# Softmax row sums of an attention kernel: partial sums folded by DMA onto half of the partitions, and a product with ones over half of the columns

## The chip, the cores and the metric

One core of one Trainium2 chip. The metric is the device time of one execution in microseconds; three runs of the kernel before took 2589.92 to 2592.28 us, median 2590.79 us. The profile is of one execution that took 2589.98 us, of which the program's instructions span 2588.2 us.

## The reference

The input is `x`, 4 images of 128 channels with 64 x 64 pixels, in float32. Two layers follow each other:

```python
# layer 0: attention over the 4096 pixels of an image, 4 heads of 32 channels
x_norm = group_norm(x, 8 groups)
q, k, v = split(qkv_w @ x_norm + qkv_b), each to [image, head, pixel, 32]
attn = softmax(q @ k.T * 32 ** -0.5)          # [image, head, 4096, 4096]
x = x + proj_w @ (attn @ v) + proj_b
# layer 1: two 3x3 convolutions with 3-bit weights
out = relu(batch_norm(conv3x3(x, quantize(w1))))
out = batch_norm(conv3x3(out, quantize(w2)))
x = relu(out + x)
```

A softmax row is exp(score) divided by the sum of exp(score) over 4096 keys. The change concerns how these sums are made.

## The kernel before

Attention runs in 32 blocks, one for each image and each 512 of its queries (`FB = 512`). A block has 32 steps, one for each 128 keys. In a step, `scores` makes for two pairs of heads the scores of 128 keys (on the partitions) against 512 queries into PSUM (L425), and ScalarE writes their exponentials into one of eight buffers of the tile `p`, 128 x 4 heads x 512 (L427). `weights` multiplies them with the values into `acc`, four heads on four bands of 32 partitions (L438). The scores run ahead of the weights: an outer loop gives three half-steps of scores, then one step of weights, then three, then two.

The sums over the keys are made in two stages. First, the exponentials of all 32 steps are added element by element into one tile of the same shape, so that each partition holds the sum over its own 32 keys. For 26 steps VectorE does that, into `r` (L448 and L450). For six, those in `MOVED = (4, 9, 14, 19, 24, 28)`, a DMA issued by GpSimd does it, into the tile `rm`: the first of a block copies (L443), the others accumulate (L445). Each moves 1 MB, on all 128 partitions. In the next block, after step 1, `merge` accumulates `rm` onto `r` by one more such DMA (L471). There is one buffer of `rm`, so the first copy of a block waits for the merge of the block before.

Then `sums` adds over the 128 partitions, by a product with a matrix of ones on TensorE (L467): one for each head and each half of the columns, eight in all, each of 256 columns. It leaves the sum of a head on all 32 partitions of its band in the tile `l`, and ScalarE copies that to SBUF (`ls`, L475). One float32 product is two records in the profile.

From there `spread` sends one row of each head to 128 partitions, `invert` takes the reciprocals there and writes them to DRAM, `gather` reads them back onto the bands, and `weigh` multiplies them with the block's output; `project` and `store` end the block.

`schedule` says after which step of the next block each of these parts is put out. Its `slots` are every third step; one visit to a slot puts other work between two groups of attention products. The sums of a block take slot 3, or slots 3 and 4 with half of the columns each; in seven blocks (`full`: the six that also project two chunks of the next image, and block 1) both halves go to slot 3. The last block has no next one, and takes `sums_at_once`, which multiplies `rm` and `r` with ones without merging them.

GpSimd issues, in program order on one queue, these accumulating DMAs as well as the stores of the projected keys, queries and values of the next image to DRAM (`kd`, `qd`, `vd`, L340 and L359) and of finished blocks (`y`, L525). A wait of one of them holds all that come after it. [...]

Of the kernel before, what the change touches and what calls it, by code (L numbers as in the profile page):

```python
# [16 lines left out]
F32 = mybir.dt.float32  # L17
AF = mybir.ActivationFunctionType
ALU = mybir.AluOpType
# [3 lines left out]
P = 128  # L23
GROUP = 16
HEADS = 4
D = 32
TAPS = 9
FB = 512
# [50 lines left out]
def _fast_body(ctx, tc, x, norm_w, norm_b, qkv_wt, qkv_b, proj_wt, proj_b,  # L79
               w1, alpha1, gamma1, beta1, w2, alpha2, gamma2, beta2, out, cnt):  # L80
    nc = tc.nc
# [10 lines left out]
    const = ctx.enter_context(tc.tile_pool(name="const", bufs=1))  # L92
# [19 lines left out]
    nc.scalar.activation(warm, mhalf, AF.Exp)  # L112
    ones = const.tile([P, D], F32, name="ones")
    nc.gpsimd.memset(ones, 1.0)
    worst = const.tile([P, FB // D], F32, name="worst")
    nc.gpsimd.memset(worst, 0.0)
    nw, nb = column(norm_w, "nw"), column(norm_b, "nb")
# [84 lines left out]
    dram = ctx.enter_context(tc.tile_pool(name="dram", bufs=1, space=bass.MemoryType.DRAM))  # L202
    kpool = ctx.enter_context(tc.tile_pool(name="kpool", bufs=NB + 1))
    pss = ctx.enter_context(tc.tile_pool(name="pss", bufs=3, space=PSUM))
    psa = ctx.enter_context(tc.tile_pool(name="psa", bufs=2, space=PSUM))
# [3 lines left out]
    att = ExitStack()  # L209
    vpool = att.enter_context(tc.tile_pool(name="vpool", bufs=NB + 1))  # L210
    qpool = att.enter_context(tc.tile_pool(name="qpool", bufs=2))
    stage = att.enter_context(tc.tile_pool(name="stage", bufs=1))
    xpool = att.enter_context(tc.tile_pool(name="xpool", bufs=3))
    ppool = att.enter_context(tc.tile_pool(name="ppool", bufs=8))
    rpool = att.enter_context(tc.tile_pool(name="rpool", bufs=1))
    sums = att.enter_context(tc.tile_pool(name="sums", bufs=2))
    wpool = att.enter_context(tc.tile_pool(name="wpool", bufs=1))

    def stack_tile(name):
# [8 lines left out]
    def load_x(b, j):  # L228
        t = xpool.tile([P, FB], F32, name=f"x{b}_{j}", tag="x")
        nc.sync.dma_start(out=t, in_=x_chunk(b, j))  # L230
        return t
# [64 lines left out]
    def banded(out, w, x):  # L296


        for c in range(HEADS):
            cs = slice(c * D, (c + 1) * D)  # L300
            nc.tensor.matmul(out[cs, :], w[:, cs], x, start=True, stop=True)  # L301
# [107 lines left out]
    pts, acc, rsum, msum = {}, {}, {}, {}  # L409
    MOVED = (4, 9, 14, 19, 24, 28)  # L410
# [20 lines left out]
    def weights(step):  # L431
        n, kt = divmod(step, NK)
        v = vs[blocks[n][0], kt // KB]
        pt = pts[step]
        if kt == 0:
            acc[n] = psa.tile([P, FB], F32, name=f"acc{n}", tag="a")
        for h in range(HEADS):
            nc.tensor.matmul(acc[n][h * D : (h + 1) * D, :], v[:, kt % KB, h * D : (h + 1) * D],  # L438
                             pt[:, h, :], start=(kt == 0), stop=(kt == NK - 1))
        if kt in MOVED:  # L440
            if kt == MOVED[0]:
                msum[n] = rpool.tile([P, HEADS, FB], F32, name=f"rm{n}", tag="rm")
                nc.gpsimd.dma_start(out=msum[n], in_=pt)  # L443
            else:
                nc.gpsimd.dma_start(out=msum[n], in_=pt, accum_op=ALU.add)  # L445
        elif kt == 1:
            rsum[n] = sums.tile([P, HEADS, FB], F32, name=f"r{n}", tag="r")
            nc.vector.tensor_tensor(rsum[n], pts[step - 1], pt, ALU.add)  # L448
        elif kt > 1:
            nc.vector.tensor_tensor(rsum[n], rsum[n], pt, ALU.add)  # L450

    def finish_parts(n):

        b, qb = blocks[n]
        av = rpool.tile([P, FB], F32, name=f"av{n}", tag="av")
        rc = rpool.tile([P, FB], F32, name=f"rc{n}", tag="rc")
        t = {}

        def copy():
            nc.scalar.copy(av, acc[n])  # L460


        def total(r, first, end, cs=slice(0, FB)):
            if "l" not in t:
                t["l"] = psa.tile([P, FB], F32, name=f"l{n}", tag="a")
            for h in range(HEADS):
                nc.tensor.matmul(t["l"][h * D : (h + 1) * D, cs], ones, r[:, h, cs],  # L467
                                 start=first, stop=end)

        def merge():  # L470
            nc.gpsimd.dma_start(out=rsum[n], in_=msum[n], accum_op=ALU.add)  # L471

        def evacuate():
            t["ls"] = stage.tile([P, FB], F32, name=f"ls{n}", tag="ls")
            nc.scalar.copy(t["ls"], t["l"])  # L475

        def sums(i):
            total(rsum[n], True, True, slice(i * FB // 2, (i + 1) * FB // 2))
            if i == 1:
                evacuate()  # L480


        def sums_at_once():
            total(msum[n], True, False)
            total(rsum[n], False, True)
            evacuate()
            for j in range(4):
                cs = slice(j * P, (j + 1) * P)
                nc.vector.reciprocal(rc[:, cs], t["ls"][:, cs])
            weigh()  # L490
            most = [small.tile([P, 1], F32, name=f"most{i}") for i in range(2)]
            for u, m in zip((t["ls"], rc), most):
                nc.vector.tensor_reduce(m, u, AX.X, ALU.max)
                nc.vector.tensor_tensor(worst[:, 0:1], worst[:, 0:1], m, ALU.add)

        def spread():
            t["lq"] = rpool.tile([P, FB // D], F32, name=f"lq{n}", tag="lq")
            nc.sync.dma_start(out=t["lq"], in_=t["ls"][0:P:D, :])  # L500

        def invert():
            t["rq"] = rpool.tile([P, FB // D], F32, name=f"rq{n}", tag="rq")
            nc.vector.reciprocal(t["rq"], t["lq"])
            t["rd"] = dram.tile([HEADS, FB], F32, name=f"rd{n}")
            nc.sync.dma_start(out=t["rd"].rearrange("h (j c) -> (h j) c", c=FB // D), in_=t["rq"])
            nc.vector.tensor_tensor(worst, worst, t["lq"], ALU.add)
            nc.vector.tensor_tensor(worst, worst, t["rq"], ALU.add)

        def gather():  # L510
            nc.sync.dma_start(out=rc, in_=t["rd"].unsqueeze(1).to_broadcast([HEADS, D, FB]))

        def weigh():
            nc.vector.tensor_tensor(av, av, rc, ALU.mult)

        def residual():
            t["x"] = load_x(b, qb)

        def project():
            t["o"] = psa.tile([P, FB], F32, name=f"po{n}", tag="a")  # L520
            banded(t["o"], wp, av)

        def store():
            nc.vector.scalar_tensor_tensor(t["x"], t["o"], bp, t["x"], ALU.add, ALU.add)
            nc.gpsimd.dma_start(out=y0[b][:, qb * FB : (qb + 1) * FB], in_=t["x"])  # L525

        return dict(copy=copy, merge=merge, sums=sums, sums_at_once=sums_at_once, spread=spread, invert=invert, gather=gather,
                    weigh=weigh, residual=residual, project=project, store=store)

# [64 lines left out]
    def schedule(n, before):  # L594
        b, qb = blocks[n]
        todo = []
        slots = [kt for kt in range(NK - 1) if (n * NK + kt) % 3 == 0]
        two = b + 1 < B and qb in (2, 3)
        full = two or n == 1

        def add(kt, f):
            todo.append((kt, f))

        def visit(kts, first, second, evacuate=None):
            add(kts[0], first)
            add(kts[-1], second)
            if evacuate:
                add(kts[-1] + 1, evacuate)

        if before:  # L610
            add(1, before["merge"])
            kts = slots[3:4] if full else slots[3:5]
            visit(kts, lambda: before["sums"](0), lambda: before["sums"](1))
            kt = kts[-1]
            add(kt + 1, before["spread"])
            add(kt + 3, before["invert"])
            add(kt + 4, before["gather"])
            add(kt + 6, before["residual"])
            add(slots[9] - 2, before["weigh"])
            add(slots[9], before["project"])  # L620
            add(slots[9] + 1, before["store"])
# [69 lines left out]
    def run_weights(count):  # L691
        for _ in range(min(count, steps - at["step"])):
            n, kt = divmod(at["step"], NK)
            if kt == 0:
                assert not todo
                todo[:] = schedule(n, parts.get(n - 1))
            weights(at["step"])
            at["step"] += 1
            if kt == NK - 2:
                parts[n] = finish_parts(n)  # L700
            if kt == NK - 1:
                parts[n]["copy"]()
            else:
                side(kt)
# [135 lines left out]
    for b in range(B):  # L840
        for j in range(4):
            y = res[b, j]
            cs = slice(j * HN, (j + 1) * HN)
# [462 lines left out]
```

## Time and profile before

| | |
|---|---|
| median of 3 runs | 2590.79 us |
| TensorE busy | 2517.2 us, 97% of the span |
| VectorE busy | 2140.3 us, 83% |
| ScalarE busy | 2081.9 us, 80% |
| GpSimd busy | 281.4 us, 11% |
| attention | to about 2270 us; then the convolutions |
| accumulating DMAs on `rm` (L445) | 160, 7.9 us from issue to landing, median of all 192 on `rm` |
| merging DMAs (L471) | 31, 7.1 us |
| product with ones (L467) | 504 records, 37.9 us of TensorE |

Busy time is the time in which an engine has at least one instruction under way, so instructions that overlap count once; a mean duration is that of one instruction alone. Behind the bar, a group shows the idle time of its engine just before its instructions, and who ended most of it. The share of a DMA queue is the time that its packets took, over 16 DMA engines and the stretch looked at.

### The profile page before, as it was taken

To read this page: it belongs to the slowest core of one execution; us is meant where nothing else is said; L and a number is where in the kernel's file an instruction comes from. 1 tells how busy PE (TensorE), PEld (TensorE's weight loads), DVE (VectorE), ACT (ScalarE), POOL (GpSimd) and SP (SyncE) were. 2 spreads that over 40 slices of the span, in tenths; PEclk is the share of its full clock that TensorE was granted. 3 is DMA by queue.
4 is the path that set the end of the run, shared out by engine and by line. 5 is a ranking of instruction groups with operands and counts; after the bars stand their busy time and mean duration, and the time that the engine had idled before them with its cause. 6 is when DMAs were issued, how large, how long until landed. Compare 5 with 4: busy or idle time off the path is not lost.

```text
span 2588.2 us, 48399 instructions
## 1 busy us (share of the span) xinstructions
PE 2517.2 (97%) x20394; PEld 1223.4 (47%) x20394; DVE 2140.3 (83%) x1402; ACT 2081.9 (80%) x2275; POOL 281.4 (11%) x456
## 2 busy tenths in 40 slices
PE   6999999999999999999999999999999999999894
PEld 3444444444444444444444444444444444477773
DVE  5898888888988898888988988888999998953344
ACT  4888899999988999999988899999889898911223
POOL 2111111111011111110011111110000000100000
PEclk9999999999999999999999999999999999999997
DMA  5876766698667767697667666986655757634004
GB/s 160 191 187 172 177 161 149 154 206 201 162 148 178 178 155 171 149 225 171 160 171 161 164 159 150 207 202 142 151 130 126 154 126 148 146 80 145 1 1 164
DMA packets 147417, 400.04 MB, mean 155 GB/s; under 512 B 59240, under 2 KB 60008, under 8 KB 118648
## 3 DMA queue, kind: packets, MB, share of 16 engines
q0 software_dynamic: 45888, 280.59, 47.9%
q1 hardware_dynamic: 100728, 115.23, 16.8%
q8 instruction: 162, 2.65, 0.4%
q10 hardware_dynamic: 576, 1.05, 0.1%
q14 instruction: 63, 0.52, 0.1%
HBM read 105.32 MB, written 55.83 MB: 62 GB/s over the span
## 4 chain that ended last, share of the span: by engine, by line
PE 88%; DVE 5%; issue 3%; DMA 2%; ACT 1%; POOL 0%; SPq 0%; DVEq 0%; POOLq 0%; ACTq 0%
PE s L425 39%; PE acc L438 34%; PE c L722 9%; DVE r L450 3%; DMA rm<-p 2%; PE l L467 1%; PE po L301 1%; PE pk L301 1%; PE pq L301 1%; PE pv L301 1%; ACT p L427 1%; DVE res L844 1%; DMA xh<-in_x_dram 0%; DMA q<-qst 0%; DVE st L570 0%
## 5 line engine op out<-in xcount | busy, mean ns | idle before, releaser
L427 ACT ACTIVATE p<-s 128x1024 f32<-128x1024 f32 x2048 | 1940.2, 1034 | 235.0 <-PE s L425 158.7
L450 DVE TENSOR_TENSOR r<-r,p 128x2048 f32<-128x2048 f32 x768 | 1758.4, 2290 | 97.3 <-ACT p L427 48.1
L425 PE MATMUL s<-q,k 64*128 64x512 f32 x8192 | 1162.3, 413 | 3.9 <-ACT p L427 2.2
L438 PE MATMUL acc<-p,v 128*32 128x512 f32 x8192 | 1021.1, 601 | 0.6 <-DVE v L355 0.6
L425 PEld LDWEIGHTS s<-q,k 64*128 64x128 f32 x8192 | 711.7, 185 | 631.9 <-issue 298.0
L438 PEld LDWEIGHTS acc<-p,v 128*32 128x32 f32 x8192 | 198.6, 109 | 453.7 <-issue 446.3
L445 POOL DMA_DIRECT2D rm<-p x160 | 138.6, 866 | 950.7 <-ACT p L427 783.6
L775 ACT COPY cv<-c 128x512 f32<-128x512 f32 x64 | 37.6, 587 | 220.8 <-DVE st L774 220.8
L722 PE MATMUL c<-hi,wq 128*128 128x512 f32 x576 | 150.1, 405 | 8.3 <-DVE hi L805 6.8
L722 PE MATMUL c<-lo,wq 128*128 128x512 f32 x576 | 148.1, 402 | 0.0
L774 DVE BATCH_NORM_STATS2 st<-c 128x6 f32<-128x512 f32 x64 | 44.7, 699 | 124.5 <-PE c L722 102.5
L722 PEld LDWEIGHTS c<-hi,wq 128*128 128x128 f32 x576 | 109.4, 191 | 40.1 <-issue 8.9
L722 PEld LDWEIGHTS c<-lo,wq 128*128 128x128 f32 x576 | 109.0, 189 | 28.9
L448 DVE TENSOR_TENSOR r<-p,p 128x2048 f32<-128x2048 f32 x32 | 73.3, 2291 | 25.0 <-ACT p L427 25.0
L336 DVE SCALAR_TENSOR_TENSOR kst<-pk,b,kst 128x512 fp32r<-128x512 f32 x32 | 24.0, 751 | 73.2 <-ACT kst L335 73.2
L336 DVE SCALAR_TENSOR_TENSOR qst<-pq,b,qst 128x512 fp32r<-128x512 f32 x32 | 24.0, 750 | 41.6 <-ACT qst L335 41.6
L471 POOL DMA_DIRECT2D r<-rm x31 | 26.3, 848 | 159.8 <-PE s L425 91.9
L340 POOL DMA_DIRECT2D qd<-qst x31 | 23.3, 753 | 177.6 <-DVE qst L336 130.2
L443 POOL DMA_DIRECT2D rm<-p x32 | 17.8, 556 | 223.3 <-ACT p L427 136.4
L335 ACT ACTIVATE kst<-pk,b 128x512 fp32r<-128x512 f32 x32 | 22.4, 701 | 21.7 <-PE pk L301 21.7
L340 POOL DMA_DIRECT2D kd<-kst x28 | 20.6, 734 | 167.6 <-DVE kst L336 159.6
L467 PE MATMUL l<-r,ones 128*32 128x256 f32 (+1 forms) x504 | 37.9, 383 | 0.5 <-issue 0.5
(129 smaller groups left out, 672.0 us busy)
## 6 DMA issues: line engine op xcount, KB each, us to landing
rm<-p POOLq DMA_DIRECT2D x192, 1024.0 KB, 7.9
q<-qd SPq DMA_DIRECT2D x248, 128.0 KB
r<-rm POOLq DMA_DIRECT2D x31, 1024.0 KB, 7.1
x<-in_x_dram SPq DMA_DIRECT2D x80, 256.0 KB
k<-kd SPq DMA_DIRECT2D x124, 128.0 KB
qd<-qst POOLq DMA_DIRECT2D x31, 512.0 KB, 6.9
kd<-kst POOLq DMA_DIRECT2D x28, 512.0 KB, 4.0
y<-x POOLq DMA_DIRECT2D x32, 256.0 KB, 5.0
```

Of the source, the lines that this page charges most:

```text
L301: nc.tensor.matmul(out[cs, :], w[:, cs], x, start=True, stop=True)
L336: nc.vector.scalar_tensor_tensor(lo, ps[what], bias, t[:, 0, :], ALU.add, ALU.subtract)
L340: (nc.sync if start else nc.gpsimd).dma_start(out=dst[b, j].rearrange("s p n -> p s n"), in_=t)
L425: nc.tensor.matmul(s[:, i, :], k[r, half, c0 : c0 + P], q[r, half, part, :], start=(part == 0), stop=(part == 1))
L427: nc.scalar.activation(pts[step][:, 2 * half : 2 * half + 2, :], s, AF.Exp, scale=SCALE)
L438: nc.tensor.matmul(acc[n][h * D : (h + 1) * D, :], v[:, kt % KB, h * D : (h + 1) * D], pt[:, h, :], start=(kt == 0), stop=(kt == NK - 1))
L445: nc.gpsimd.dma_start(out=msum[n], in_=pt, accum_op=ALU.add)
L448: nc.vector.tensor_tensor(rsum[n], pts[step - 1], pt, ALU.add)
L450: nc.vector.tensor_tensor(rsum[n], rsum[n], pt, ALU.add)
L467: nc.tensor.matmul(t["l"][h * D : (h + 1) * D, cs], ones, r[:, h, cs], start=first, stop=end)
L722: nc.tensor.matmul(ps[:, j, :].rearrange("p (r w) -> p r w", w=W), w[:, tap, :], part[:, j * RB + kh : j * RB + kh + RB, kw : kw + W], sta ...
L774: nc.vector.bn_stats(st[:, b * NB + c, :], ps[:, j, :])
```

## The change

The partial sums of the DMAs no longer keep the shape of `p`. Their new tile `f` has 128 partitions and two blocks of 512 columns in place of four: the lower 64 partitions hold heads 0 and 2, the upper 64 hold heads 1 and 3, and each partition holds the sum of two partitions of `p`. `fold` brings a tile there in four DMAs of 256 KB (64 partitions, two heads): first each half of the partitions with its own two heads, then each half of the partitions from the other one. The second two of a fold wait for the first two. `f` has two buffers. `merge` now folds `r` into `f` in the same way, where it added `rm` onto `r` before.

With two heads on two halves of the partitions, one product of 256 columns with `pair` (ones in the upper left and the lower right quarter, zeros elsewhere) makes the sums of two heads at a time. Four products, one to a band, make all sums of a block: a band holds two heads, 16 partitions each, for one half of the columns. So the copy to `ls` has 256 columns, `spread` takes one row out of every 16 partitions, and the reciprocals come back in two transfers. All blocks make their sums in one visit, at slot 3. The last block multiplies `f` with `hones` (ones on one half of the partitions) and `r` with `ones`.

```diff
+    hones = const.tile([P, 2, D], F32, name="hones")
+    pair = const.tile([P, D], F32, name="pair")
+    for t in (hones, pair):
+        nc.gpsimd.memset(t, 0.0)
+    for i in range(2):
+        r = slice(i * P // 2, (i + 1) * P // 2)
+        nc.gpsimd.memset(hones[r, i, :], 1.0)
+        nc.gpsimd.memset(pair[r, i * D // 2 : (i + 1) * D // 2], 1.0)
...
+    fpool = att.enter_context(tc.tile_pool(name="fpool", bufs=2))
...
         if kt in MOVED:
-            if kt == MOVED[0]:
-                msum[n] = rpool.tile([P, HEADS, FB], F32, name=f"rm{n}", tag="rm")
-                nc.gpsimd.dma_start(out=msum[n], in_=pt)
-            else:
-                nc.gpsimd.dma_start(out=msum[n], in_=pt, accum_op=ALU.add)
+            fold(n, pt)
...
+    def fold(n, t):
+        new = n not in msum
+        if new:
+            msum[n] = fpool.tile([P, 2, FB], F32, name=f"f{n}", tag="f")
+        rows = [slice(i * P // 2, (i + 1) * P // 2) for i in range(2)]
+        for first in (True, False):
+            for r in range(2):
+                src = t[rows[r if first else 1 - r], r::2, :]
+                if new and first:
+                    nc.gpsimd.dma_start(out=msum[n][rows[r]], in_=src)
+                else:
+                    nc.gpsimd.dma_start(out=msum[n][rows[r]], in_=src, accum_op=ALU.add)
...
         def merge():
-            nc.gpsimd.dma_start(out=rsum[n], in_=msum[n], accum_op=ALU.add)
+            fold(n, rsum[n])
...
-        def sums(i):
-            total(rsum[n], True, True, slice(i * FB // 2, (i + 1) * FB // 2))
-            if i == 1:
-                evacuate()
+        def sums():
+            l = psa.tile([P, FB], F32, name=f"l{n}", tag="a")
+            for c in range(4):
+                f, i = divmod(c, 2)
+                nc.tensor.matmul(l[c * D : (c + 1) * D, : FB // 2], pair,
+                                 msum[n][:, i, f * FB // 2 : (f + 1) * FB // 2],
+                                 start=True, stop=True)
+            t["ls"] = stage.tile([P, FB], F32, name=f"ls{n}", tag="ls")
+            nc.scalar.copy(t["ls"][:, : FB // 2], l[:, : FB // 2])
...
-            nc.sync.dma_start(out=t["lq"], in_=t["ls"][0:P:D, :])
+            nc.sync.dma_start(out=t["lq"], in_=t["ls"][0 : P : D // 2, : FB // 2])
...
-            nc.sync.dma_start(out=rc, in_=t["rd"].unsqueeze(1).to_broadcast([HEADS, D, FB]))
+            for f in range(2):
+                nc.sync.dma_start(out=rc[:, f * FB // 2 : (f + 1) * FB // 2],
+                                  in_=t["rd"][f].unsqueeze(1).to_broadcast([HEADS, D, FB // 2]))
...
-            kts = slots[3:4] if full else slots[3:5]
-            visit(kts, lambda: before["sums"](0), lambda: before["sums"](1))
-            kt = kts[-1]
+            kt = slots[3]
+            add(kt, before["sums"])
```

More of the change, by code (lines that the diff above doesn't have):

```diff
@@ L460, in copy, with merge, sums_at_once @@
             nc.scalar.copy(av, acc[n])
-        def total(r, first, end, cs=slice(0, FB)):
-            if "l" not in t:
-                t["l"] = psa.tile([P, FB], F32, name=f"l{n}", tag="a")
-            for h in range(HEADS):
-                nc.tensor.matmul(t["l"][h * D : (h + 1) * D, cs], ones, r[:, h, cs],
-                                 start=first, stop=end)
-        def merge():
-            nc.gpsimd.dma_start(out=rsum[n], in_=msum[n], accum_op=ALU.add)
-        def evacuate():
-            t["ls"] = stage.tile([P, FB], F32, name=f"ls{n}", tag="ls")
-            nc.scalar.copy(t["ls"], t["l"])
-        def sums(i):
-            total(rsum[n], True, True, slice(i * FB // 2, (i + 1) * FB // 2))
-            if i == 1:
-                evacuate()
[L483 to L486, printed above, removed]
+        def merge():
+            fold(n, rsum[n])
[8 more added lines that the diff above has]
+            nc.scalar.copy(t["ls"][:, : FB // 2], l[:, : FB // 2])
+        def sums_at_once():
+            l = psa.tile([P, FB], F32, name=f"l{n}", tag="a")
+            for h in range(HEADS):
+                nc.tensor.matmul(l[h * D : (h + 1) * D, :], hones[:, h % 2, :], msum[n][:, h // 2, :],
+                                 start=True, stop=False)
+            for h in range(HEADS):
+                nc.tensor.matmul(l[h * D : (h + 1) * D, :], ones, rsum[n][:, h, :],
+                                 start=False, stop=True)
+            t["ls"] = stage.tile([P, FB], F32, name=f"ls{n}", tag="ls")
+            nc.scalar.copy(t["ls"], l)
             for j in range(4):
@@ L504, in invert @@
             nc.vector.reciprocal(t["rq"], t["lq"])
-            t["rd"] = dram.tile([HEADS, FB], F32, name=f"rd{n}")
-            nc.sync.dma_start(out=t["rd"].rearrange("h (j c) -> (h j) c", c=FB // D), in_=t["rq"])
+            t["rd"] = dram.tile([2, HEADS, FB // 2], F32, name=f"rd{n}")
+            nc.sync.dma_start(out=t["rd"].rearrange("f h (j c) -> (f h j) c", c=FB // D), in_=t["rq"])
             nc.vector.tensor_tensor(worst, worst, t["lq"], ALU.add)
@@ L598, in schedule @@
         two = b + 1 < B and qb in (2, 3)
-        full = two or n == 1
         def add(kt, f):
```

## The prediction

> **What bounds the kernel now.** I read the page first (busy shares, then the chain that ended last), then busy time by stretch, then the order of time on TensorE around the row sums, and last the tile `rm` and the DMA queues over short stretches.
>
> The page: shares, chain, groups.
>
> ```profile
> PE 2517.2 (97%) x20394; PEld 1223.4 (47%) x20394; DVE 2140.3 (83%) x1402; ACT 2081.9 (80%) x2275; POOL 281.4 (11%) x456
> ...
> PE 88%; DVE 5%; issue 3%; DMA 2%; ACT 1%; POOL 0%; SPq 0%; DVEq 0%; POOLq 0%; ACTq 0%
> ...
> L427 ACT ACTIVATE p<-s 128x1024 f32<-128x1024 f32 x2048 | 1940.2, 1034 | 235.0 <-PE s L425 158.7
> ...
> L445 POOL DMA_DIRECT2D rm<-p x160 | 138.6, 866 | 950.7 <-ACT p L427 783.6
> ...
> L467 PE MATMUL l<-r,ones 128*32 128x256 f32 (+1 forms) x504 | 37.9, 383 | 0.5 <-issue 0.5
> ```
>
> Busy time by stretch, from the middle of attention:
>
> ```profile
> 300.00:700.00 400.00, 400.00 (x3422) 179.30 (x3416) 353.01 (x194) 363.11 (x395) 46.97 (x62) 1.00 0.75 176
> 1500.00:1900.00 400.00, 399.54 (x3346) 176.50 (x3342) 358.80 (x221) 362.06 (x392) 43.36 (x57) 1.00 0.72 164
> ```
>
> TensorE has no gap, ScalarE and VectorE have about a tenth free, and the DMA engines are taken for about 0.73 of the time. So a product taken off TensorE shortens attention, as long as nothing else fills up.
>
> TensorE in order of time, one visit that makes all sums of a block and one that makes half of them:
>
> ```profile
> 767.64 1.06 PE L438 MATMUL acc<-p,v 128*32 128x512 f32 x8
> 768.52 1.05 PE L467 MATMUL l<-r,ones 128*32 128x256 f32 x16
> 769.50 1.66 PE L425 MATMUL s<-q,k 64*128 64x512 f32 x12
> ...
> 1740.98 0.61 PE L467 MATMUL l<-r,ones 128*32 128x256 f32 x8
> 1741.53 1.67 PE L425 MATMUL s<-q,k 64*128 64x512 f32 x12
> ```
>
> The pipe gives 0.98 us (768.52 to 769.50) to 16 records and 0.55 us (1740.98 to 1741.53) to 8.
>
> The tile `rm` (the time of its DMAs to landing, and who waited for it):
>
> ```profile
>   ACT p L427: 4.1, 5
> ...
> DMA to landing us min/median/max: 4.4/7.8/14.6
> ```
>
> The DMA queues: first over 300 to 2200 us, then 745.9 to 754 us (one accumulating transfer alone), 754 to 761 us (one plain one alone), and 22.6 to 23.15 us (start-up copies from 32 partitions of SBUF to 32 others). Columns: packets, MB, share of 16 engines.
>
> ```profile
> q0 software_dynamic: 37682, 237.04, 55.6%
> q1 hardware_dynamic: 52023, 73.76, 15.2%
> ```
>
> ```profile
> q0 software_dynamic: 144, 1.05, 64.4%
> ...
> r<-rm POOLq DMA_DIRECT2D x1, 1024.0 KB, 7.6
> ```
>
> ```profile
> q0 software_dynamic: 144, 1.05, 38.8%
> ...
> rm<-p POOLq DMA_DIRECT2D x1, 1024.0 KB, 4.6
> ```
>
> ```profile
> q1 hardware_dynamic: 48, 0.07, 48.8%
> ```
>
> 64.4% of 8.1 us is 5.2 us of all 16 engines for 1 MB accumulated; 38.8% of 7 us is 2.7 us for 1 MB copied. Accumulating costs twice a copy[...]. 128 data packets of 8 KB make 0.34 us a packet for the copy, 0.085 us for each 2 KB. The start-up copies moved 32 packets of 2 KB: 48.8% of 0.55 us times 16, over 32, is 0.134 us each, 1.6 times as long.
>
> [...] 16 engines times 2 KB in 0.134 us is 245 GB/s, against 385 GB/s at 0.085 us. [...] No transfer of the kernel before shows an accumulation on half of the partitions.
>
> **The change part by part.**
>
> *Products removed.* Sums of 31 blocks go from eight products (16 records) to four (8 records). Seven blocks ("full": six with two chunks, and block 1) did them in one visit and save 0.98 - 0.55 = 0.43 us each, 3.0 us. The other 24 did them in two visits of 0.55 us and save one, 13.2 us. All lies on TensorE, which sets the end: -16.2 us. The last block has as many products as before.
>
> *ScalarE copy of `ls`.* Half the columns of a 0.6 us copy, 31 times: about 9 us on an engine with a tenth free. Nothing.
>
> *Constants, spread, gather.* Six more small memsets at the start, of 0.1 to 0.2 us as those beside them, ahead of `nw` and `wqkv`, which the program needs some 14 us later. The reciprocals travel as before in 8 KB; they are read back by two transfers instead of one, and `weigh` comes about twelve steps (some 27 us) later. Nothing.
>
> *Waits on TensorE.* The sums now wait for two landings, and stand where the first half stood before, which needed the merged tile as well.
>
> *The DMA sums.* Each fold (six per block, and the merge) was one transfer of 1 MB; it is four of 256 KB, in two phases. Phase A adds a half onto itself: source and destination both on 64 partitions. Phase B adds the other half, and waits for A's landing. Bytes are the same. GpSimd issues four: between 0.5 (start-up) and 0.85 us each, so up to 3.4 us of a fold interval of some 10 us: no bound by itself. In order of time:
>
> - A reads 512 KB per transfer[...] 2.1 us at the measured 245. The lower bound is the engines' own 1.3 us (5.2 / 4). I take 2.2.
> - B reads its source from one half and its destination from the other: 1.3 us if they interleave[...]. [...]I take 1.4.
> - A fold is 2 x 2.2 + 2 x 1.4 = 7.2 us of all engines in place of 5.2 (from 5.2 to 9.6).
> - 300 to 2200 us holds 27 blocks of 7: 189 folds. 2.0 us more each is 378 of 1900 us, 20 points: DMA share from 71 to 91%. It fits, with little left.
>
> Latency: from issue the first packet comes after about 1.4 us. A1 stands behind A0 on the same engines; with one part in seven for other traffic (5.2 us of data plus about 1.9 fixed is 7.1, the median is 7.8), A0 ends at 3.9 us and A1 at 6.4; B0, issued at about 4.2, follows A1 at once and ends at 8.0; B1, issued at 6.6, ends at 9.6. About 10 us to landing in place of 7.8. A probability tile has eight buffers: with 6.9 us per three steps and a visit (768.52 to 775.41) it is written again 18 us after its exps start, some 15.5 us after they end. So 5 us of room stay, less what GpSimd is behind. Queued behind the waiting phase B on GpSimd are the stores of k, q, v and y: up to 6 us later, and needed by loads many steps later. The chain itself can start a fold every 8 us or so, and folds come every 9 to 11. The merge is issued at 746.11 and the sums stand at 768.52: 22 us for 10. One wait goes away: two buffers of `f` mean that the first fold of a block no longer waits for the merge.
>
> I charge 3 us for folds that come late in the blocks with the most stores. Sum: -16.2 + 3 = -13 us, **2577.5 us**.
>
> **Rivals.**
>
> *DMA full.* If A takes 2.4 and B 1.8, a fold is 8.4 us and the share 71 + 189 x 3.2 / 19 = 103%. Then folds set the pace of attention (2200 us): 3% over, and bubbles between phases on top, +65 to +100 us less the 16 gained: about 2660. If B too takes 2.4: 71 + 44 = 115%, 2900. [...]
>
> *Room for p used up.* Folds fit on average, but GpSimd runs behind where stores, merge and fold meet; ScalarE then waits for a landing (before: 4.1 us in all, 5 times), and TensorE for ScalarE. Some 1 us for each of 30 to 45 of 223 folds: 2605 to 2620. For it: the longest landing was already 14.6 us of 15.5. Against it: the median has 5 us left.
>
> *No change.* ScalarE's wait and TensorE's gain cancel, 2590. Narrow.
>
> **How the numbers follow.** Forecast 0.50, room used up 0.20, DMA full 0.23, no change 0.07. Faster is the forecast alone: 0.50. Slower is two rivals: 0.43. The range starts under the full 16 us with a little from ScalarE, 2569, and takes in the room rival and the lower part of the full one, to 2680; some 0.12 stay above it, for A and B both near 2.4.
>
> **What would show it.** Right: `l` with 8 records a block (about 250), near 0.55 us for each; folds landing in about 10 us from their first issue; ScalarE waiting for `f` under 15 us in all; DMA share about 0.9 between 300 and 2200 us; TensorE without gaps. Wrong: ScalarE waiting for `f` by hundreds of us, TensorE with gaps before `s`, DMA share at 1.0 and folds landing later and later in a block. If the share stays near 0.75, [...] my A is too high.

## The result, and the profile after

The changed kernel takes 2846.87 us (median of 4 runs, 2843.37 to 2855.29), the kernel before 2590.85 us (4 runs) in the same session: a ratio of 1.099 with a 95% interval of 1.097 to 1.102. It is 256 us slower, where 13 us less were forecast.

The page of the changed kernel: busy shares, the chain that ended last, and two of its groups.

```profile
PE 2594.7 (91%) x20146; PEld 1221.0 (43%) x20146; DVE 2143.3 (75%) x1402; ACT 2075.0 (73%) x2275; POOL 947.4 (33%) x1131
...
DMA 53%; PE 28%; issue 10%; POOL 4%; ACT 3%; DVE 2%; SPq 0%; POOLq 0%; ACTq 0%; DVEq 0%
DMA f<-p 49%; PE s L435 10%; PE acc L448 8%; PE c L743 8%; DMA f<-r 4%; POOL f L470 3%; ACT p L437 2%; DVE r L456 1%; POOL f L468 1%; DVE res L865 1%; PE po L311 0%; PE pk L311 0%; PE pq L311 0%; PE pv L311 0%; DMA wqkv<-in_L_conv_qkv_w_dram 0%
...
L435 PE MATMUL s<-q,k 64*128 64x512 f32 x8192 | 1208.1, 421 | 182.3 <-ACT p L437 178.8
L470 POOL DMA_DIRECT2D f<-p x704 | 684.0, 977 | 1343.9 <-DMA f<-p 1219.5
```

Before, the chain was TensorE for 88% and DMA for 2%. Now DMA is 53%, nearly all of it `f<-p`, the folds (one fold is the four transfers that bring one tile into `f`). GpSimd stands 1219.5 us in front of accumulating transfers, waiting for the landing of an earlier one, and TensorE stands 178.8 us in front of scores because ScalarE has not freed a PSUM tile.

Busy time by stretch, the same two as before the change:

```profile
300.00:700.00 400.00, 369.68 (x3076) 160.81 (x3072) 315.27 (x174) 321.96 (x352) 152.62 (x168) 0.97 0.91 158
1500.00:1900.00 400.00, 368.39 (x3074) 161.25 (x3068) 311.70 (x172) 318.56 (x348) 151.19 (x166) 0.96 0.91 156
```

All three compute engines have lost some 8 to 13% of their busy time in each stretch, so none of them sets the pace. The DMA engines are at 0.91, not at 1. The DMA queues of 300 to 2200 us agree with 73.9 and 14.9%:

```profile
q0 software_dynamic: 105532, 214.67, 73.9%
q1 hardware_dynamic: 50096, 68.86, 14.9%
```

How the wait travels, in the list of waits of the whole program (who waited for whom, us in total, times, longest):

```profile
POOL f L470 <- DMA f<-p: 1255.6, 593, 6.7
...
ACT p L437 <- DMA f<-p: 211.4, 72, 9.5
...
PE s L435 <- ACT p L437: 178.8, 101, 9.1
```

GpSimd issues a fold late because the fold before has not landed; the tile of `p` that it reads is therefore released late; ScalarE, which wants to write that buffer again, waits (before: 4.1 us in 5 waits); TensorE waits for ScalarE.

A0 and A1 are the two transfers of a fold's first phase, A, and B0 and B1 those of its second, each written to the same half as the A of its number. From each transfer's issue and landing, a fold looks like this in the median: A0 is issued at 0 and lands at 5.3 us; B0, which waits for it, is issued at 5.66 and lands at 9.76; the next fold of the block, whose A0 waits for that, starts at 10.25. In the mean, which is what counts over a block, A0 lands after 5.7 us, B0 goes out 0.3 us later and lands after 4.6 more, and the next A0 goes out 0.5 us after that: 11.1 us from fold to fold. Seven of them are 78 us; before, a block took 67 to 73 us from the third on (from its first exps to those of the next). That the mean is the chain's own length, and not a pace set elsewhere, shows in how seldom it breaks: of 222 folds that follow another, 172 were issued within 0.7 us of the landing of the B0 before them, and 28 sooner, each the first of its block, which writes the other buffer of `f`; only 22 came later. Before, 94 of 222 were issued so soon after a landing, and folds came 10.0 us apart in the mean.

So GpSimd falls behind. In the median of the 192 folds of `p` it issued A0 5.0 us after the exps that the fold reads had ended (before, 0.6 us), and the whole fold had landed 17.9 us after these exps (before, 9.0). The prediction had counted some 15.5 us until the buffer of `p` is written again.

Of the 31 blocks compared, 27 got 3 to 14 us longer. In blocks 7, 15 and 23 (counted from 0) the DMA engines also load the next image's keys and values; these got 20, 22 and 13.5 us longer.

### The profile page after: what moved, and what is told of

The parts are those of the page before. It is cut to its first block, busy times and chain, and to the rows that moved or that the text cites. A ratio compares the mean times of both kernels' runs of the same rounds, so it can differ in the third digit from the quotient of the medians.

```text
span 2842.5 us, 49017 instructions
## 1 busy us (share of the span) xinstructions
PE 2594.7 (91%) x20146; PEld 1221.0 (43%) x20146; DVE 2143.3 (75%) x1402; ACT 2075.0 (73%) x2275; POOL 947.4 (33%) x1131
## 4 chain that ended last, share of the span: by engine, by line
DMA 53%; PE 28%; issue 10%; POOL 4%; ACT 3%; DVE 2%; SPq 0%; POOLq 0%; ACTq 0%; DVEq 0%
DMA f<-p 49%; PE s L435 10%; PE acc L448 8%; PE c L743 8%; DMA f<-r 4%; POOL f L470 3%; ACT p L437 2%; DVE r L456 1%; POOL f L468 1%; DVE res L865 1%; PE po L311 0%; PE pk L311 0%; PE pq L311 0%; PE pv L311 0%; DMA wqkv<-in_L_conv_qkv_w_dram 0%
## 5 line engine op out<-in xcount | busy, mean ns | idle before, releaser
L435 PE MATMUL s<-q,k 64*128 64x512 f32 x8192 | 1208.1, 421 | 182.3 <-ACT p L437 178.8
L470 POOL DMA_DIRECT2D f<-p x704 | 684.0, 977 | 1343.9 <-DMA f<-p 1219.5
L448 PE MATMUL acc<-p,v 128*32 128x512 f32 x8192 | 1063.2, 623 | 2.2 <-DVE x L547 1.6
L470 POOL DMA_DIRECT2D f<-r x124 | 120.6, 976 | 188.4 <-DMA f<-r 135.9
L795 DVE BATCH_NORM_STATS2 st<-c 128x6 f32<-128x512 f32 x64 | 44.7, 699 | 124.7 <-PE c L743 101.9
L559 POOL MEMSET t<- 128x18 f32 x32 | 5.9, 184 | 177.1 <-PE c L743 107.6
L468 POOL DMA_DIRECT2D f<-p x64 | 51.0, 977 | 0.2 <-issue 0.2
L350 POOL DMA_DIRECT2D kd<-kst x28 | 29.1, 1039 | 29.5 <-DVE kst L346 28.8
L350 POOL DMA_DIRECT2D qd<-qst x31 | 33.0, 1076 | 11.7 <-DVE qst L346 11.7
```

Of the source, the lines that this page charges most:

```text
L350: (nc.sync if start else nc.gpsimd).dma_start(out=dst[b, j].rearrange("s p n -> p s n"), in_=t)
L435: nc.tensor.matmul(s[:, i, :], k[r, half, c0 : c0 + P], q[r, half, part, :], start=(part == 0), stop=(part == 1))
L468: nc.gpsimd.dma_start(out=msum[n][rows[r]], in_=src)
L470: nc.gpsimd.dma_start(out=msum[n][rows[r]], in_=src, accum_op=ALU.add)
L795: nc.vector.bn_stats(st[:, b * NB + c, :], ps[:, j, :])
```

## The experiments

Two theories, each seeming enough by itself. P, partitions: a transfer that reads both inputs of its addition, source and destination, from one half of the partitions is slow. C, chain: the second phase of a fold waits for the first, and that puts two issues and two landings in a row. A third, S, is that many small transfers cost as such. Each run stood beside a run of the kernel before on the same chip; where no interval is given, it is one run, and differences are tens of us.

**All partitions.** Only the slices in `fold` change:

```diff
-                src = t[rows[r if first else 1 - r], r::2, :]
+                src = t[:, r if first else r + 2, :]
...
-                    nc.gpsimd.dma_start(out=msum[n][rows[r]], in_=src, accum_op=ALU.add)
+                    nc.gpsimd.dma_start(out=msum[n][:, r, :], in_=src, accum_op=ALU.add)
```

> The same four transfers of 256 KB in a fold, the same two phases with the same wait between them, the same 2 KB pieces; but each transfer now goes over all 128 partitions (head r of p onto column block r, then head r + 2 onto the same block). The row sums so made mix heads; number of bytes, issues, products and waits are those of the change. Theory P[...]: folds shrink from a period of 10.25 us to 7 or 8, TensorE is the bound again, 2575 to 2600 us. Theory C (chain: two phases one after the other, each with a fixed cost of issue and landing, set the length[...]): no change, 2820 to 2860 us.

Measured: 2638.42 us. Neither theory alone: transfers over all partitions take back 208 us of the 256, and 47 us are left over 2591.47. ScalarE's waits for the tile fall from 211.4 us to 44.7:

```profile
ACT p L437 <- DMA f<-p: 44.7, 15, 7.3
```

The terms of the chain are now 4.4, 0.5, 4.1 and 0.5 us in the mean (the last where a fold still waits for the one before; 97 of 222 now come later than that). Seven times 9.5 us are 66 us, which is close to a block. 19 of the 31 blocks are no longer than before, and half of the loss lies in blocks 7, 15 and 23 with their loads; in the change one block of 31 was no longer.

**Own half twice, other half twice.** `src = t[rows[r], r::2, :]` in both phases, and `src = t[rows[1 - r], r::2, :]` in both.

> Both phases of a fold read their source from the half of the partitions that they write (phase A twice); the other half's partitions are left out of the DMA sums, and their own are counted twice. P: phase B gets as slow as phase A (5.3 us from issue to landing in place of 4.1), a fold period near 11.5 to 12 us, 3000 to 3150 us. C: 2820 to 2870 us, as the change.

> Both phases read their source from the other half (phase B twice)[...]; each half's own partitions are left out of the DMA sums. P: phase A gets as fast as phase B (4.1 us), a fold period near 9 us, 2600 to 2700 us. C: 2820 to 2860 us, as the change.

Measured: 3074.73 us and 2684.94 us, as P has it in both. Between 300 and 2200 us the median 2 KB packet on GpSimd's queue took 336 ns with the own half, 191 with the other half, 187 over all partitions. So reading two inputs from one half is slow, and reading one from each half costs almost nothing in the packets. Folds started 12.1, 10.4 and 10.2 us apart in the mean, against 11.1 in the change and 10.0 before. Most of what the halves cost is in phase A: without it, 162 of the 208 us are gone.

**No wait between the phases.** Phase B adds onto a tile of its own:

```diff
+            cross[n] = gpool.tile([P, 2, FB], F32, name=f"g{n}", tag="g")
...
-        for first in (True, False):
+        for dst, first in ((msum[n], True), (cross[n], False)):
```

> Phase B adds onto a tile of its own, so that it no longer waits for phase A; same transfers from and to the same halves. The tile of phase B is left out of the row sums. The first phase B of a block is a copy, which saves a little. P alone: the transfers take what they took, the engines stay full, 2780 to 2850 us. C: the chain per fold is half as long (5 us in place of 10), TensorE is the bound again, 2575 to 2620 us. Something in between says that the wait costs because it comes on top of slow transfers.

The lines left out write `dst` in place of `msum[n]`, and let the first phase B of a block be a copy.

Measured: 2613.96 us. The same slow transfers, from and to the same halves, cost 22 us over the kernel before when a phase does not wait for the other. Its busy time by stretch:

```profile
300.00:700.00 400.00, 395.59 (x3344) 174.92 (x3340) 347.37 (x192) 356.36 (x388) 165.83 (x184) 1.00 0.95 171
1500.00:1900.00 400.00, 398.28 (x3320) 175.03 (x3320) 357.79 (x214) 360.79 (x394) 163.89 (x181) 1.00 0.94 167
```

The DMA engines are busier here (0.95) than in the change (0.91), and TensorE is nearly full. So it was not the DMA engines' share that held the change up: they could carry these transfers at almost the old pace, though one in fourteen is a copy here that is an addition in the change. Nor was it the length of one fold: from first issue to last landing it took 12.4 us in the median here, and 12.2 in the change.

**Both remedies.** All partitions, and the second phase on its own tile.

> Both remedies at once, to complete the two by two: all 128 partitions in each transfer, and the second phase on a tile of its own, so nothing waits within a fold (the sums mix heads, and the second tile is left out of them). Products, number of issues, bytes and pieces are those of the change. [...] the gain of the products alone, 2576 to 2584 us. If four issues a fold, or something else of the change, costs as well: 2590 us or more.

Measured: 2582.80 us, ratio 0.997 (0.996 to 0.998), within 4 us of the products alone (below). That completes the two by two:

| | phase B waits for phase A | no wait |
|---|---|---|
| halves of the partitions | 2847 (the change) | 2614 |
| all partitions | 2638 | 2583 |

From the lower right, the halves alone add 31 us, the wait alone 56, both together 264, three times their sum. The numbers above fit one reading: with the wait alone seven folds need 66 us, which most blocks have and those with more traffic do not; with halves and wait they need 78, which hardly any has. ScalarE's waits for landings go the same way: 6 us with neither, 25 with the halves alone, 45 with the wait alone, 211 with both.

**Four transfers, no phases.** The kernel before, each 1 MB transfer cut into four of one head each:

```diff
-                nc.gpsimd.dma_start(out=msum[n], in_=pt, accum_op=ALU.add)
+                for h in range(HEADS):
+                    nc.gpsimd.dma_start(out=msum[n][:, h, :], in_=pt[:, h, :], accum_op=ALU.add)
```

> The kernel before with each 1 MB transfer cut into four of 256 KB, one for each head, on all 128 partitions; no second phase, nothing waits within a fold, old products. If four issues and 2 KB pieces cost by themselves (theory S): 2610 to 2640 us, as much as full ports with two phases did. If the wait between phases is what costs there: 2588 to 2598 us, as before.

Measured: 2591.41 us, beside 2591.21. S falls: four issues and 2 KB pieces are hidden here, although GpSimd is busy for 147 us of 400 in place of 47.

**The products alone.** The old transfers and merge, the new products on the merged tile:

```diff
-                                 msum[n][:, i, f * FB // 2 : (f + 1) * FB // 2],
+                                 rsum[n][:, i, f * FB // 2 : (f + 1) * FB // 2],
```

> The kernel before, its transfers of 1 MB and its merge, with the new products alone: four of 256 columns in one visit, on the merged tile's first two heads (heads 2 and 3 and the upper half's share are left out of the sums), and the shorter copy and the new spread and gather. It measures what the product is worth with nothing lost to the transfers. If TensorE sets the pace: 16 us less, 2573 to 2578 us. If ScalarE or VectorE already share the pace: 2583 to 2592 us.

Measured: 2579.13 us, ratio 0.9953 (0.9937 to 0.997): 12 us less, with an interval of 8 to 16. The tile `l` in this run:

```profile
L481 PEld LDWEIGHTS l<-r,pair x248: 105/110/111, 138.2 to 2213.0; 128*32 128x32 f32 x124
L481 PE MATMUL l<-r,pair x248: 376/379/404, 138.2 to 2213.2; 128*32 128x256 f32 x124
```

248 records are eight for each of 31 blocks. Before, there were sixteen for each, 496, and eight of the last block under the same line, 504. Most blocks are 0.2 to 0.4 us shorter than before.

**Four folds in place of six.** `MOVED = (4, 11, 18, 25)`, and VectorE adds two more steps of a block.

> The change with four folds for the steps of a block in place of six (steps 4, 11, 18, 25), so five with the merge; VectorE adds the two others, 2.3 us each. If a block waits for the sum of its folds (about 10 to 11 us each): five are 55 us of 69, TensorE sets the pace again, and the products' gain shows in part, 2574 to 2600 us. If each fold on its own is too long for the eight buffers of p: stalls shrink only by a third, 2720 to 2780 us.

Measured: 2640.84 us, ratio 1.020 (1.018 to 1.022): 206 us of the 256 are gone. That is between the two expectations, nearer to the first: fewer folds free the block, but 50 us stay. A single fold is as long as in the change (11.9 us in the median to its last landing, 12.2 there), so what was cured is the queue of folds and not the fold. ScalarE's waits for `f` fall from 211 to 19 us. This line, and the chain of this run, which names what took over:

```profile
ACT p L437 <- DMA f<-p: 19.0, 11, 5.2
...
PE 61%; DVE 14%; DMA 10%; issue 9%; POOL 2%; ACT 2%; SPq 0%; DVEq 0%; POOLq 0%; ACTq 0%
```

VectorE, with 64 additions more, is 14% of the chain; in the change it was 2%. Whether its additions are all of the 50 us was not tried. As folds are now 14 us apart in the median, this run has folds that stand alone, and one shows what a fold is made of. GpSimd in order of time, 671 to 684 us:

```profile
671.60 1.96 POOL L470 DMA_DIRECT2D f<-p  x2 [3.55 <-ACT p L437]
676.81 0.96 POOL L470 DMA_DIRECT2D f<-p  x1 [3.26 <-DMA f<-p]
679.74 0.96 POOL L470 DMA_DIRECT2D f<-p  x1 [1.96 <-DMA f<-p]
```

And what the DMA engines moved from 671.6 to 683.5 us, in 40 slices of 0.30 us:

```profile
DMA  0000099996999978999997599999410079999300
GB/s 0 0 0 0 0 117 96 103 96 62 89 110 96 96 124 117 110 96 96 89 110 83 69 131 151 179 193 165 83 21 14 0 96 165 172 200 193 55 0 0
...
q0 software_dynamic: 576, 1.05, 71.7%
```

A0 and A1 are issued in one go at 671.60. The first byte moves 1.5 us later (slice 5). The two take until slice 22, 5.4 us for 0.52 MB at about 100 GB/s moved, so 200 GB/s read if the two inputs of each addition are counted, with the engines at 9 tenths or so. A0 landed at 676.53, A1 at 679.45. B0 goes out at 676.81, when A0 has landed, and moves at up to 190 GB/s as A1 ends. B1 goes out only when A1 has landed, and so late that the engines stand idle for two slices. The last byte moves 11.3 us after the first issue and B1 lands at 11.7; before, 1 MB in one transfer landed in 7.8 in the median.

**Fold once.** Old transfers and merge, then one fold of the merged tile for a block, after step 5 of the next, products at slot 4 (complete sums):

```diff
+            nc.gpsimd.dma_start(out=fsum[n][rows[r]], in_=t[rows[r], r::2, :])
+        for r in range(2):
+            nc.gpsimd.dma_start(out=fsum[n][rows[r]], in_=t[rows[1 - r], r::2, :], accum_op=ALU.add)
...
+            add(5, before["once"])
+            kt = slots[4]
```

> The transfers of 1 MB and the merge as before the change; then, once for a block, one fold of the merged tile (two copies of a half, two accumulations from the other half), issued after step 5 of the next block, and the four products at slot 4 in place of slot 3. Complete sums. If what hurt the change is that every fold of a block is a chain of two slow phases: one such chain in 70 us has room, and the gain of the products shows, 2574 to 2582 us. If halves of the partitions hurt wherever they are used, or the queue of GpSimd is held too long: 2590 to 2620 us.

Measured: 2594.35 us, ratio 1.0012 (1.0005 to 1.0019). That is in the slower range, at its lower end, and no gain. From the first exps of one block to those of the next, 18 blocks were 0.2 to 0.4 us shorter than before, as with the products alone; the loss is in a few blocks (block 8: +5.7 us, 17: +3.1, 23: +3.5). In block 8 ScalarE waited 5.0 us for a landing in `rm`; over the program these waits are 12.1 us, 4.1 before. What holds the other blocks was not tried.

**Copy and add, and the fold on VectorE.** The merged tile's other half copied by two plain transfers of SyncE (`nc.sync.dma_start`) or by VectorE (`nc.vector.tensor_copy`), and the own half added by VectorE after it:

```diff
+            f = fsum[n][rows[r]]
+            nc.vector.tensor_tensor(f, f, t[rows[r], r::2, :], ALU.add)
```

> A version meant to keep the gain: transfers and merge as before the change; after step 5 of the next block SyncE copies the other half of the merged tile by two plain transfers, after step 8 VectorE adds each half's own part (two additions of 64 partitions by 1024), products at slot 3. Complete sums. If the loss of the single fold per block came from accumulating transfers and their wait on GpSimd's queue: 2578 to 2585 us. If VectorE's additions or the copies come late for slot 3: 2588 to 2605 us.

> As the run with copy and add, but VectorE does the copy across the halves too (two copies and two additions of 64 partitions by 1024 after step 7), and no transfer is added at all. Complete sums. VectorE has a tenth of its time free, 7 us a block, and the fold takes 3.5 to 4.5 us of it. If that is free: 2578 to 2585 us. If VectorE holds up the tiles of p by it: 2585 to 2610 us.

Measured: 2671.42 us, ratio 1.031 (1.030 to 1.033), and 2673.46 us, ratio 1.032 (1.030 to 1.034), slower than either expectation. In the first, the products stood waiting for these additions, as the tile `l` shows, while VectorE was not waiting for the copies: it stood 4.7 us before all 62 additions.

```profile
  DVE f L473: 117.5, 43
...
L473 DVE TENSOR_TENSOR f<-f,r 64x1024 f32<-64x1024 f32 x62 | 75.4, 1216 | 4.7 <-DMA f<-r 3.8
```

So VectorE came to these additions late because it was busy with others. A tenth of free time on average was no free time at that place.

> Copy and add as before, with the products at slot 4 (steps 12 to 14) in place of slot 3 (steps 9 to 11). In the first version the products stood waiting for VectorE's additions (117 us in 43 waits), while blocks in which slot 3 falls on step 11 lost nothing. If that deadline is the whole of its loss: 2580 to 2588 us, under both kernels. If VectorE's 2.4 us a block or the two copies cost wherever the products stand: 2592 to 2630 us.

Measured: 2619.04 us, ratio 1.011 (1.009 to 1.013). With the products one slot later these waits are gone from the tile `l`, and 52 us with them; 27 us over the kernel before remain, in blocks 1, 16, 23, 26 and 28 above all. What holds these was not tried. No version beat the kernel before with complete sums.

## Why the prediction was wrong

*TensorE as the bound, and the products: right in kind, a quarter too large.* The products were put at -16.2 us; alone they measured -12, with an interval that reaches -8 and -16. I had 0.43 or 0.55 us for a block, and most blocks of that run are 0.2 to 0.4 us shorter; why not more was not looked into. Records 248 for about 250, 0.61 us to eight as before.

*Four issues, start-up constants, `spread` and `gather`: right.* Four small transfers alone cost nothing (2591.41 us), and the products with their new spread and gather kept their gain. An issue of a half took longer than the 0.5 to 0.85 us I gave it, 0.96 us.

*Transfers within one half: right in kind, too small in size, and the share came out by luck.* I took 2.2 us for a transfer of phase A, near the 2.1 us at the 245 GB/s of the start-up packets, and 1.4 for phase B, an estimate a little above the 1.3 us of the engines; the lone fold shows 2.7 and 1.6 to 1.8. From the mean packet of 245 ns, 512 to a fold and 16 engines, a fold took 7.8 us of all engines, not 7.2. DMA share was forecast at 91%, and the queues add up to 89, but with 171 folds between 300 and 2200 us in place of the 189 that I counted. The start-up packets gave the direction, but too high a rate: about 200 GB/s was read in phase A of the lone fold. There the two transfers of the phase landed one after the other: A1 was issued 0.6 us after A0 and landed 2.9 us after it, about one transfer's 2.7 us.

*The step that failed: "The chain itself can start a fold every 8 us or so, and folds come every 9 to 11."* Folds did have to come every 10.0 us, but the chain starts one every 11.1 us in the mean (10.25 in the median; the shortest was 8.3). The terms: A0 lands after 5.7 us where I had 3.9; then 0.3 us until B0 goes out, as I had; B0 takes 4.6 us to land, where I had 3.8; and 0.5 us more to the next A0, for which I had nothing. Even the fold that stands alone shows 4.9 us for A0: its data took 2.7 us and not 2.2, and from last byte to landing took 0.4 us (measured at B1), for which my 3.9 has no room. Each term is off by a little, all to the same side, and they stand in one line: nothing else of the fold runs in their place. I had compared folds with their spacing in single pairs and called 8 against 9 room. Over a block of 69 us, seven at 8 are 56 us; seven at 11.1 are 78.

*The 3 us for late folds* was the term that this broke: it is 256 + 12, some 270 us. I charged folds that come late now and then, and expected the queue to catch up. A chain that is longer than its block doesn't catch up. Of the five us of room that I counted for a buffer of `p`, GpSimd's delay alone, 5.0 us in the median, took all, and a fold landed 12.2 us after its first issue where I had about 10.

*One of the signs misled.* "DMA share about 0.9" was to show me right, and 1.0 wrong. It came out at 0.9 with the forecast wrong, and the run without the wait had 0.95 and was 233 us faster. The signs that told were TensorE without gaps, ScalarE's waits for `f` under 15 us (211) and folds landing in about 10 us (12.2): all three failed.

*The rivals.* "DMA full" with both phases at an assumed 2.4 us gave 2900, near the time, but for a reason that the runs contradict: phase B was not slow (191 ns a packet where both phases are like it), and the engines had room (0.95 without the wait). "Room for p used up" had the way of the damage right (ScalarE for `f`, TensorE for ScalarE), at a tenth of its size. Neither named the chain that made folds late in every block.

## What to carry to other kernels

Before splitting one accumulating transfer into phases that wait for each other, add up issue, first byte, data and landing along the phases that wait, and multiply by their number in a block: that sum, not the DMA engines' share, has to stay well under the block's time. Here 66 us of 69 still lost 47 us, and 78 lost 256. An accumulation whose two inputs lie in one half of the partitions is no small transfer: its packets took 336 ns against 187 over all partitions. And an engine's average free time says nothing of the place where a short addition is to go: one slot later for the products that needed it was worth 52 us.

## What was unexpected of the hardware

- An accumulating transfer of 256 KB took GpSimd 0.96 us to issue on 64 partitions with two pieces each and 0.85 on 128 partitions with one piece, no less than the whole 1 MB before (0.85).
- Accumulating packets of 2 KB took 187 ns in the median over all partitions, somewhat more than a quarter of the 636 ns of 8 KB: small pieces by themselves lost some 18%, which stayed hidden; from one half alone they took 336.
- The clock that TensorE was granted was lower in the runs in which it waited more: 0.99 over the span before, 0.96 in the change, 0.94 with the own half twice. A record of the scores took 421 ns in the mean, 413 before. What this added to the time was not separated from the waits.
